# Group norm of the element after next, moved beside layer 1's last products

## The chip, the cores and the metric

The kernel runs on one core of a Trainium2 chip. A time is the device time of one execution in microseconds (us). The core has a matmul engine (PE, with a separate record of its weight loads, PEld), a vector engine (DVE), a scalar engine (ACT), a general engine (POOL) and a queue that issues the transfers (SP). Each engine works through its own list of instructions in order and waits on semaphores for the others. Matmuls write to PSUM, a small accumulation memory that PE, DVE and ACT use; everything else lies in SBUF, and the inputs and outputs in HBM.

## What is computed

The input x has 8 elements of 512 channels and 32 x 32 = 1024 positions, all in 32-bit floats. Two attention layers follow each other, element by element:

```python
# layer 0
hn  = group_norm(x, gn1_scale, gn1_bias)          # 32 groups of 16 channels
qkv = einsum('bchw,oc->bohw', hn, w_qkv) + b_qkv   # 8 heads of 64 channels
wgt = softmax(einsum('bct,bcs->bts', q * scale, k * scale))
a   = einsum('bts,bcs->bct', wgt, v)
x   = x + group_norm(einsum('bchw,oc->bohw', a, w_proj) + b_proj, gn2_scale, gn2_bias)
# layer 1: weights normalised by row, one head of 512 channels
qkv = einsum('oc,bcn->bon', w_qkv, x)
qkv = qkv / (sqrt(mean(qkv**2, axis=1)) + 0.0001)
attn = softmax(einsum('bci,bcj->bij', q, k) * C ** -0.5)
h   = einsum('oc,bcn->bon', w_out, einsum('bij,bcj->bci', attn, v))
out = (x + h) * 2 ** -0.5
```

The change concerns the first line, the group norm that makes `hn`, and where its work is done.

## The kernel before

Channels lie on the 128 partitions in 4 blocks (`CI` = 4), positions along the free dimension in two halves of 512 (`HN`). A matmul of 128 x 128 by 128 x 512 in 32-bit floats is recorded as two passes. The kernel keeps the order in which the program is written on every engine (`InOrder`, lines 26 to 34): nothing is reordered by a planner, and each engine's list is the order of the calls in the text.

The main loop (line 1012) goes over the elements b. Each starts with 32 **steps** of layer 0's heads (lines 1015 to 1058). A step i handles 128 query positions of two heads and is written in `Heads.step` (line 490): first the softmax of step i on DVE, ACT and POOL; then on PE, in odd steps from step 5 on, the values of an earlier pair of steps; then the step's *fill*, which in even steps is a piece of the projection of the next two heads' queries and keys (`project_rows`, tile `pqk`); then the scores of step i + 1 (tile `s`). After that come the transpose of the step before (`turn`, tile `pb`), its four transfers to `pT`, the work called *early*, the scaling by the sums (POOL), and the work called *later*.

Scores are made in halves: two heads of 64 channels each use half the rows of PE's array and run beside each other. One tile of scores is 128 x 1024 and fills two PSUM banks. The pool `ps_s` (line 101) has three such tiles, handed out in turn, two for each step; so the second head's scores of step i + 1 take the tile of the first head's scores of step i, once that head's exponential has read it. The pool `ps_m` (line 102) has two tiles of one bank, also in turn, for the values (`po`), the projection (`pqk`) and the small matmuls of the norms.

After the 32 steps, layer 0 is finished (`finish_layer0`), and layer 1 of the element is computed (`Layer1.project`, then `products`). Layer 1 ends with eight *products*: for each half `th` of the positions and each channel block c, eight matmuls of the weights e with the values v (`po<-e,v`, line 882), followed by `keep` (line 888), which on DVE divides by the softmax sums and adds x, and for the second half issues the output transfer. The four products of the first half stand by themselves (lines 1086 to 1092). The four of the second half are the fills of steps 0 to 3 of the next element's heads, ahead of the projection's piece where there is one (line 1097), and their `keep` is in the steps' later part.

The **norm** that makes `hn` of element b + 1 is spread over the heads of element b (lines 1034 to 1052): the four loads of 512 KB from HBM in steps 4 to 7, eight statistics on DVE in steps 6 to 13, their aggregation in step 14, then `GroupNorm.all_steps` one piece per step: a small matmul `pm` that averages over the groups, four small operations on DVE, a small matmul `pv` for the variance, and 17 small operations for the reciprocal root, the scale `a` and the offset `c`. POOL applies them to the four blocks in steps 21 and 22. `hn` of b + 1 is first read in step 24.

Large buffers are seven slots (`Slots`, line 37), handed out in the order in which they came free.

Of the kernel before, what the change touches and what calls it, by code (L numbers as in the profile page):

```python
# [13 lines left out]
P = 128  # L14
# [4 lines left out]
G1S, G1B, BQ, BK, BV, BP, G2S, G2B, GQKV, GOUT, NCOLS = 0, 4, 8, 12, 16, 20, 24, 28, 32, 44, 48  # L19
# [33 lines left out]
def attention_blocks_kernel(  # L53
# [26 lines left out]
    B, C, H, W = x.shape  # L80
    N = H * W
    NH, D, GROUPS = 8, C // 8, 32
    CI, NT, HN = C // P, N // P, N // 2
# [20 lines left out]
    PE, VE, AC, PO, SY = (InOrder(tc, e) for e in (nc.tensor, nc.vector, nc.scalar, nc.gpsimd, nc.sync))  # L104

    def big(name, lead=CI):

        return slots.take([P, lead, CI * N // lead], name)

    def wide(name):  # L110
        return ps_s.tile([P, 2, HN], F32, tag="sc", name=name)

    def bank(name, n=HN):
        return ps_m.tile([P, n], F32, tag="mm", name=name)

    def matmuls(pm, terms):

        for k, (lhsT, rhs) in enumerate(terms):
            PE.matmul(pm, lhsT, rhs, start=(k == 0), stop=(k == len(terms) - 1))
            if k % 2:  # L120
                yield

    def run(pieces):
        for _ in pieces:
            pass
# [4 lines left out]
    x0 = big("hn_0")  # L130
# [19 lines left out]
    def load_x(b, xt, ci):  # L150
        SY.dma_start(out=xt[:, ci, :], in_=xv[b, :, ci, :])
# [42 lines left out]
    def rsqrt_steps(r, v, n, name):  # L194

        t = small.tile([P, 4 * CI], F32, tag="rs_t", name=f"rs_{name}")[:, :n]
        VE.tensor_scalar(r.bitcast(I32), v.bitcast(I32), -0.5, 1597463007.0, ALU.mult, ALU.add)
        yield
        for _ in range(3):
            VE.tensor_mul(t, r, v)  # L200
            VE.tensor_mul(t, t, r)
            VE.tensor_scalar(t, t, -0.5, 1.5, ALU.mult, ALU.add)
            VE.tensor_mul(r, r, t)
            yield
# [29 lines left out]
    def fetch(name, b):  # L234
        SY.dma_start(out=place(name, b), in_=far[name])
# [19 lines left out]
    class GroupNorm:  # L255


        def __init__(self, mv, n, g0, b0, name):
            self.mv, self.n, self.g0, self.b0, self.name = mv, n, g0, b0, name

        def new(self, tag):
            return small.tile([P, CI], F32, tag=f"gn_{tag}", name=f"{tag}_{self.name}")[:, : self.n]

        def mean_steps(self):
            mv, n = self.mv, self.n
            pm = bank(f"pm_{self.name}")
            PE.matmul(pm[:, :n], gavg, mv[:, :, 0], start=True, stop=True)
            yield

            self.mean, self.d = self.new("mean"), self.new("d")  # L270
            VE.tensor_copy(self.mean, pm[:, :n])
            VE.tensor_sub(self.d, mv[:, :, 0], self.mean)
            VE.tensor_mul(self.d, self.d, self.d)
            VE.tensor_add(self.d, self.d, mv[:, :, 1])
# [3 lines left out]

        def coeff_steps(self):
            n = self.n  # L280
            pv = bank(f"pv_{self.name}")
            PE.matmul(pv[:, :n], gavg, self.d, start=True, stop=True)
            yield
            ve, self.a, self.c = self.new("ve"), self.new("a"), self.new("c")
            VE.tensor_scalar_add(ve, pv[:, :n], EPS)
            yield from rsqrt_steps(self.a, ve, n, self.name)
            VE.tensor_mul(self.a, self.a, cols[:, self.g0 : self.g0 + n])
            VE.tensor_mul(self.c, self.mean, self.a)
            VE.tensor_sub(self.c, cols[:, self.b0 : self.b0 + n], self.c)
# [10 lines left out]
    class Norm1:  # L300


        def __init__(self, b, xt):
            self.b, self.xt = b, xt
            self.st = small.tile([P, CI, 2, 6], F32, tag="gn_st1", name=f"st1_{b}")
            self.mv = small.tile([P, CI, 2], F32, tag="gn_mv1", name=f"mv1_{b}")
            self.gn = GroupNorm(self.mv, CI, G1S, G1B, f"1_{b}")

        def stats(self, ci, k):
            gn_stats(self.st[:, ci], self.xt[:, ci, :], k)  # L310
# [413 lines left out]
    class Layer1:  # L724
# [154 lines left out]
            PE.matmul(pe, root2, self.sums[th], start=True, stop=True)  # L879
            VE.reciprocal(self.sums[th], pe)  # L880

        def products(self, th, c):
            self.po = bank(f"po1_{self.b}_{th}_{c}")
            e = self.e[th]

            run(matmuls(self.po, [(self.v[:, t, c * P : (c + 1) * P], e[:, t, :]) for t in (0, 4, 1, 5, 2, 6, 7, 3)]))

        def keep(self, th, c):

# [54 lines left out]
    norm1 = Norm1(0, x0)  # L944
# [46 lines left out]
    v0_0 = big("v0_0", NT)  # L991
# [6 lines left out]
    qk0, todo = project_qk(0, 0, x0)  # L998
# [6 lines left out]
        slots.give(name)  # L1005


    heads = Heads(0, x0, v0_0, qk0)
    fills = [[lambda: next(v0)] for _ in range(CI)]
    laters = [[] for _ in range(CI)]  # L1010
    heads.scores(0)
    for b in range(B):
        hn, more = heads.hn, b + 1 < B
        todo = iter(())
        for i in range(STEPS):
            j, r = divmod(i, NB)
            due = []
            fill = [lambda: due.append(next(todo, None))] if (i - LAG) % RG else []
            early, later = [], []
            if i < CI:  # L1020
                fill, later = fills[i] + fill, laters[i]
            if r == 0:
                if j + 1 < CI:
                    heads.qk[j + 1], todo = project_rows(b, j + 1, hn)
                elif more:
                    qk_next, todo = project_rows(b + 1, 0, hn_next)
                if j + 1 == CI:
                    slots.give(f"hn_{b}")
                    if not more:
                        o_last = big(f"o_{b}")  # L1030
                        todo = project_out_half(b, heads, o_last)
            later.append(lambda: [f() for f in due if f])

            if more:


                if i == CI:
                    hn_next = big(f"hn_{b + 1}")
                    norm1 = Norm1(b + 1, hn_next)
                if 0 <= i - CI < CI:  # L1040
                    later.append(lambda: load_x(b + 1, hn_next, i - CI))
                if 0 <= i - CI - 2 < 2 * CI:
                    later.append(lambda: norm1.stats((i - CI - 2) // 2, i % 2))
                k = i - 3 * CI - 2
                if k == 0:
                    coeffs = norm1.gn.all_steps()
                    early += [norm1.aggregate, lambda: next(coeffs)]
                elif 0 < k < 8:
                    early.append(lambda: next(coeffs, None))
                if 0 <= k - 7 < CI // 2:  # L1050
                    for ci in range(2):
                        later.append(lambda ci=ci: norm1.apply(2 * (k - 7) + ci, PO))

            if i == STEPS - NB + 1:
                xt = big(f"x_{b}")
            if 0 <= i - (STEPS - NB + 1) < CI:
                later.append(lambda: load_x(b, xt, i - (STEPS - NB + 1)))
            heads.step(i, fill, early, later)

        if more:  # L1060
            v0_next = big(f"v0_{b + 1}", NT)
            v0 = project_v0(b + 1, hn_next, v0_next)
            next(v0)
        heads.values(STEPS // RG - 2)
        heads.turn()
        if more:
            fetch("proj7", b)
            ta = big(f"ta_{b}").rearrange("p (k i) (h n) -> p k i h n", k=2, h=2)
            rhs = RightSide(heads.a, ta[:, 0], ta[:, 1])
            for j in range(CI // 2 + 1):  # L1070
                rhs.sums(j)
            for _ in range(3):
                next(v0)
        else:
            fetch("score", b)
            begun = OutBegun(b, heads)
        heads.values(STEPS // RG - 1)
        slots.give(f"v0_{b}")
        if more:
            finish_layer0(b, heads, rhs, xt, v0)  # L1080
        else:
            finish_last(b, heads, xt, o_last, begun)
        fetch("value", b)
        one = Layer1(b, xt)
        one.project()
        for c in range(CI):
            one.products(0, c)
            if c == 0:
                one.total(0)
            one.keep(0, c)  # L1090
            if c == 1:
                one.total(1)
        slots.give(f"e_{b}_0")
        if more:
            heads = Heads(b + 1, hn_next, v0_next, qk_next)
            heads.scores(0)
            fills = [[lambda c=c: one.products(1, c)] for c in range(CI)]
            laters = [[lambda c=c: one.keep(1, c)] for c in range(CI)]

            def done(b=b):  # L1100
                for name in (f"v1_{b}", f"e_{b}_1", f"x_{b}"):
                    slots.give(name)

            laters[CI - 1].append(done)
        else:
            for c in range(CI):
                one.products(1, c)
                one.keep(1, c)
# [33 lines left out]
```

## Time and profile before

| | |
|---|---|
| median of 3 runs | 3293.95 us (3293.58 to 3295.57) |
| the profiled execution | 3295.35 us |
| its span, first to last instruction | 3293.2 us |
| granted clock of PE | 0.997 |
| busy: PE, DVE, ACT, POOL | 3263.8, 2118.5, 1071.5, 983.4 us |
| DVE, one statistic of 128 x 512 | 0.67 us |
| POOL, norm applied to one block of 128 x 1024 | 1.19 us |
| DVE, reciprocal of the sums, 128 x 512 | 3.35 us |
| load of one block of hn, issue to landing | 6.1 us |

A row of the profile names the engine, the operation, what is written and read (`out<-in`, buffer numbers left out), the shape and the count. `64*128` after MATMUL is a matmul that uses half of the array's rows. In an order of time each row has its start, counted from the first instruction, its length, and in brackets the idle time of the engine just before it with the releaser. Neighbouring rows of the same kind are merged (`x8`). The ends of matmuls are modelled, so the distance between the starts of two rows is the better measure of what a group costs.

### The profile page before, as it was taken

The numbers are of one execution on the slowest core, as the hardware profiler recorded it, in microseconds if no ns is written. First come the engines' busy times: TensorE is split into PE (matmuls) and PEld (weight loads), VectorE is DVE, ScalarE is ACT, GpSimd is POOL, SyncE is SP. The second block draws the span as 40 slices with busy tenths as digits, with TensorE's granted clock in tenths as the row PEclk, the third lists the DMA queues.
The fourth block names the chain that finished last, engine by engine and source line by source line (L and its number), as shares of the span: only waits on it lengthen the run. The fifth ranks groups of instructions, "written<-read, shape, count | busy, mean of one in ns | idle before, by whom it ended". The sixth has DMA issues, their size and how long they took to land.

```text
span 3293.2 us, 35605 instructions
## 1 busy us (share of the span) xinstructions
PE 3263.8 (99%) x13178; PEld 1606.6 (49%) x13178; DVE 2118.5 (64%) x2869; ACT 1071.5 (33%) x1813; POOL 983.4 (30%) x857
## 2 busy tenths in 40 slices
PE   8999999999999999999999999999999999999899
PEld 4444544545444454444544445444554545444354
DVE  4696647955488554885449754596645966468653
ACT  2453124521145211551215412254123531145210
POOL 0352123511245022460214503254122531235121
PEclk9999999999999999999999999999999999999899
DMA  5675206741078411782118811287204762057500
GB/s 189 195 196 166 81 6 179 202 150 67 8 205 212 128 45 35 209 219 91 45 53 216 233 52 44 81 219 208 77 13 125 207 177 90 13 140 196 183 7 26
DMA packets 182707, 410.82 MB, mean 125 GB/s; under 512 B 27620, under 2 KB 27656, under 8 KB 176520
## 3 DMA queue, kind: packets, MB, share of 16 engines
q1 hardware_dynamic: 182416, 408.53, 43.6%
q8 instruction: 105, 1.72, 0.2%
q14 instruction: 66, 0.54, 0.0%
q10 hardware_dynamic: 120, 0.02, 0.0%
HBM read 112.48 MB, written 27.56 MB: 43 GB/s over the span
## 4 chain that ended last, share of the span: by engine, by line
PE 94%; DVE 2%; DMA 2%; SPq 1%; issue 1%; DVEq 0%; ACTq 0%
PE po L34 26%; PE s L34 13%; PE pqk L34 12%; PE pv L34 7%; PE p_e_T L34 7%; PE p_e_B L34 5%; PE py L34 4%; PE p_u_T L34 3%; PE p_v_T L34 3%; PE p_o_T L34 3%; PE p_v_B L34 3%; PE p_u_B L34 3%; PE p_o_B L34 2%; DMA pT<-pb 1%; DVE pb L34 1%; PE pG L34 1%
## 5 line engine op out<-in xcount | busy, mean ns | idle before, releaser
L34 POOL TENSOR_SCALAR p<-p,tt 128x1024 f32<-128x1024 f32 x512 | 566.8, 1120 | 917.0 <-DVE tt L34 915.3
L34 ACT ACTIVATE p<-s,nm 128x1024 f32<-128x1024 f32 x512 | 565.9, 1110 | 839.6 <-DVE nm L34 801.1
L34 DVE TENSOR_REDUCE nm<-s 128x1 f32<-128x1024 f32 x512 | 602.1, 1217 | 180.1 <-PE s L34 179.2
L34 DVE STREAM_TRANSPOSE pb<-p 128x2048 f32<-128x2048 f32 x256 | 589.5, 2303 | 29.6 <-POOL p L34 18.8
L34 PE MATMUL s<-qk 64*128 64x512 f32 x2048 | 508.7, 602 | 0.0
L34 PE MATMUL po<-pT,v 128*64 128x256 f32 x4096 | 471.8, 383 | 3.8 <-DMA pT<-pb 2.8
L34 PE MATMUL pqk<-hn,qk 64*128 64x512 f32 (+1 forms) x2016 | 473.9, 591 | 0.0
L34 PE MATMUL po<-e,v 128*128 128x512 f32 x1024 | 450.9, 595 | 0.0
L34 PEld LDWEIGHTS po<-pT,v 128*64 128x64 f32 x4096 | 287.2, 137 | 217.1 <-ACT v L34 68.2
L34 PEld LDWEIGHTS pqk<-hn,qk 64*128 64x128 f32 (+1 forms) x2016 | 201.8, 187 | 252.1 <-issue 240.2
L34 PEld LDWEIGHTS po<-e,v 128*128 128x128 f32 x1024 | 192.2, 190 | 252.7 <-issue 245.5
L34 PEld LDWEIGHTS s<-qk 64*128 64x128 f32 x2048 | 194.4, 186 | 238.8 <-issue 234.2
L34 POOL TENSOR_TENSOR u<-u,xy 128x512 f32<-128x512 f32 x64 | 78.9, 1270 | 762.8 <-DMA xy<-far_rinv 390.2
L34 PE MATMUL pv<-v,hn 128*128 128x512 f32 x512 | 229.0, 598 | 0.0
L34 DVE TENSOR_TENSOR e<-e,p_e_T 128x512 f32<-128x512 f32 x160 | 107.0, 685 | 145.0 <-PE p_e_T L34 142.8
L34 POOL TENSOR_TENSOR qk<-qk,v 128x512 f32<-128x512 f32 x124 | 158.6, 1279 | 83.9 <-ACT v L34 83.9
L34 ACT ACTIVATE e<-e,shift,rinv 128x512 f32<-128x512 f32 x128 | 100.8, 811 | 247.7 <-DVE e L34 247.7
L34 POOL TENSOR_TENSOR esum<-esum,e 128x512 f32<-128x512 f32 x96 | 121.5, 1267 | 163.9 <-ACT e L34 161.4
L34 PEld LDWEIGHTS pv<-v,hn 128*128 128x128 f32 x512 | 94.6, 190 | 115.1 <-issue 114.8
L34 PE MATMUL p_e_T<-s,t 128*128 128x512 f32 x320 | 147.8, 592 | 0.0
L34 PE MATMUL py<-x,gram 128*128 128x512 f32 x320 | 141.6, 602 | 6.0 <-issue 6.0
L34 DVE TENSOR_TENSOR v<-po,esum 128x512 f32<-128x512 f32 x56 | 38.7, 691 | 160.0 <-PE po L34 159.8
(186 smaller groups left out, 3062.3 us busy)
## 6 DMA issues: line engine op xcount, KB each, us to landing
pT<-pb SPq DMA_DIRECT2D x1024, 256.0 KB, 4.4
hn<-in_x_dram SPq DMA_DIRECT2D x32, 512.0 KB, 6.1
x<-in_x_dram SPq DMA_DIRECT2D x32, 512.0 KB, 6.1
out_dram<-x SPq DMA_DIRECT2D x32, 512.0 KB, 3.3
score<-far_score SPq DMA_DIRECT2D x8, 1792.0 KB, 7.6
value<-far_value SPq DMA_DIRECT2D x8, 1792.0 KB, 7.0
qk<-far_qk SPq DMA_DIRECT2D x7, 2048.0 KB, 8.0
proj<-far_proj SPq DMA_DIRECT2D x7, 1792.0 KB, 9.1
```

What stands on the lines that cost most here:

```text
L34: return lambda *args, **kw: self._pin(call(*args, **kw))
```

## The change

Four things are done together.

1. For elements 2 to 7 the norm is moved out of the heads into the end of layer 1 of the element two before. After `project()`, the slot for `hn` of b + 2 is taken and its four loads are issued. The statistics and their aggregation come after the third product of the first half. The matmul `pm` is issued after half of the fourth product's matmuls, and `pv` after half of the next product's (`between`, `norm_step`). The norm of element 1 stays in the heads of element 0.
2. These small matmuls take a tile of the scores' pool (`wide`) and not of `ps_m`.
3. POOL applies the norm in steps 1, 3, 5 and 7 of the heads of element b, one block each.
4. The first product of the second half is issued before the heads of the next element begin, for every element but the last. The other three become the fills of steps 0 to 2; step 3's is empty. The slots of layer 1 are given back a step earlier.

```diff
-            pm = bank(f"pm_{self.name}")
+            pm = self.bank(f"pm_{self.name}")
...
-            pv = bank(f"pv_{self.name}")
+            pv = self.bank(f"pv_{self.name}")
...
-        def products(self, th, c):
+        def products(self, th, c, between=None):
...
-            run(matmuls(self.po, [(self.v[:, t, c * P : (c + 1) * P], e[:, t, :]) for t in (0, 4, 1, 5, 2, 6, 7, 3)]))
+            terms = [(self.v[:, t, c * P : (c + 1) * P], e[:, t, :]) for t in (0, 4, 1, 5, 2, 6, 7, 3)]
+            for k, _ in enumerate(matmuls(self.po, terms)):
+                if k == 1 and between:
+                    between()
...
-            if more:
+            if b and more and i % 2 and i < 2 * CI:
+                later.append(lambda: norm1.apply(i // 2, PO))
+            if not b:
...
         one = Layer1(b, xt)
         one.project()
+        hn_now, steps = hn_next, iter(())
+
+        def norm_step():
+            next(steps, None)
+
+        if b + 2 < B:
+
+            hn_next = big(f"hn_{b + 2}")
+            norm1 = Norm1(b + 2, hn_next, lambda name: wide(name)[:, 0])
+            for c in range(CI):
+                load_x(b + 2, hn_next, c)
+            steps = norm1.gn.all_steps()
         for c in range(CI):
-            one.products(0, c)
+            one.products(0, c, norm_step if c == CI - 1 else None)
             if c == 0:
                 one.total(0)
+            if c == 2 and b + 2 < B:
+                for ci in range(CI):
+                    for k in range(2):
+                        norm1.stats(ci, k)
+                norm1.aggregate()
+            if c == CI - 1:
+                norm_step()
             one.keep(0, c)
             if c == 1:
                 one.total(1)
         slots.give(f"e_{b}_0")
         if more:
-            heads = Heads(b + 1, hn_next, v0_next, qk_next)
+            one.products(1, 0, norm_step)
+            run(steps)
+            one.keep(1, 0)
+            heads = Heads(b + 1, hn_now, v0_next, qk_next)
             heads.scores(0)
-            fills = [[lambda c=c: one.products(1, c)] for c in range(CI)]
-            laters = [[lambda c=c: one.keep(1, c)] for c in range(CI)]
+            fills = [[lambda c=c: one.products(1, c)] for c in range(1, CI)] + [[]]
+            laters = [[lambda c=c: one.keep(1, c)] for c in range(1, CI)] + [[]]
...
-            laters[CI - 1].append(done)
+            laters[CI - 2].append(done)
```

More of the change, by code (lines that the diff above doesn't have):

```diff
@@ L255, in attention_blocks_kernel, with __init__ @@
     class GroupNorm:
-        def __init__(self, mv, n, g0, b0, name):
-            self.mv, self.n, self.g0, self.b0, self.name = mv, n, g0, b0, name
+        def __init__(self, mv, n, g0, b0, name, bank=bank):
+            self.mv, self.n, self.g0, self.b0, self.name, self.bank = mv, n, g0, b0, name, bank
         def new(self, tag):
@@ L300, in attention_blocks_kernel, with __init__ @@
     class Norm1:
-        def __init__(self, b, xt):
+        def __init__(self, b, xt, bank=bank):
             self.b, self.xt = b, xt
@@ L306, in __init__ @@
             self.mv = small.tile([P, CI, 2], F32, tag="gn_mv1", name=f"mv1_{b}")
-            self.gn = GroupNorm(self.mv, CI, G1S, G1B, f"1_{b}")
+            self.gn = GroupNorm(self.mv, CI, G1S, G1B, f"1_{b}", bank)
         def stats(self, ci, k):
@@ L1005, in attention_blocks_kernel @@
         slots.give(name)
-    heads = Heads(0, x0, v0_0, qk0)
+    heads, norm1, hn_next = Heads(0, x0, v0_0, qk0), None, None
     fills = [[lambda: next(v0)] for _ in range(CI)]
```

## The prediction

> **What bounds the kernel now.** I read the page's busy shares first, then the matmul engine's instructions in order of time around one boundary between two elements, then all engines in the same stretch.
>
> ```profile
> PE 3263.8 (99%) x13178; PEld 1606.6 (49%) x13178; DVE 2118.5 (64%) x2869; ACT 1071.5 (33%) x1813; POOL 983.4 (30%) x857
> PE 94%; DVE 2%; DMA 2%; SPq 1%; issue 1%; DVEq 0%; ACTq 0%
> ```
>
> PE is busy for all but 29 us, and those lie at the start and the end of the program. So nothing counts that does not change the number, the order or the waits of PE's instructions. PE in order of time, boundary from element 0 to element 1, steps 2 to 5 of element 1's heads (start us, length us):
>
> ```profile
> 915.85 4.12 PE L34 MATMUL pqk<-hn,qk 64*128 64x512 f32 x15
> 919.38 0.59 PE L34 MATMUL s<-qk 64*128 64x512 f32 x1
> 919.81 0.59 PE L34 MATMUL pqk<-hn,qk 64*128 64x512 f32 x1
> 919.81 2.30 PE L34 MATMUL s<-qk 64*128 64x512 f32 x7
> 922.04 7.13 PE L34 MATMUL po<-e,v 128*128 128x512 f32 x16
> 929.11 1.99 PE L34 MATMUL s<-qk 64*128 64x512 f32 x8
> 930.93 3.60 PE L34 MATMUL pqk<-hn,qk 64*128 64x512 f32 x16
> 934.36 1.88 PE L34 MATMUL s<-qk 64*128 64x512 f32 x8
> ```
>
> Step 3 is the 922.04 line: layer 1's last product (7.07 us to the next start), and then the scores of step 4. All engines in that stretch:
>
> ```profile
> 921.31 2.35 DVE L34 TENSOR_REDUCE nm<-s 128x1 f32<-128x1024 f32 x2 [3.94 <-PE s L34]
> 922.63 1.11 ACT L34 ACTIVATE p<-s,nm 128x1024 f32<-128x1024 f32 x1 [1.60 <-DVE nm L34]
> 923.58 2.30 DVE L34 STREAM_TRANSPOSE pb<-p 128x2048 f32<-128x2048 f32 x1
> ```
>
> The maximum of head 0's scores starts at 921.31, its exponential runs from 922.63 to 923.74. Scores have a ring of three PSUM tiles and two tiles per step, so the second head's scores of step 4 take the tile that this exponential empties. Today that is hidden: PE is in the product until 929.11.
>
> The norm's two small matmuls, in element 2's heads (first two lines), and the same pair for the second norm between full-array matmuls (last three):
>
> ```profile
> 989.53 0.39 PE L34 MATMUL pm<-mv,gavg 128*128 128x4 f32 x2
> 990.05 3.67 PE L34 MATMUL po<-pT,v 128*64 128x256 f32 x32
> ...
> 1128.25 0.28 PE L34 MATMUL pm<-mv,gavg 128*128 128x4 f32 x2
> 1128.39 3.68 PE L34 MATMUL pv<-v,hn 128*128 128x512 f32 x8
> 1131.90 0.28 PE L34 MATMUL pv<-d,gavg 128*128 128x4 f32 x2
> ```
>
> In the heads pm delays the next matmul by 0.52 us (990.05 - 989.53); in the full-array stretch by 0.14.
>
> [...] at 916.70 half the array waits 0.56 us for VectorE to free a bank, and no later work is taken in its place. [...] scores run as two 64-row halves, each half one pass per 0.429 us, and scores that follow a full-array product last 1.92 us up to another full-array product, 1.82 up to another 64-row stage. [...]
>
> **The change, part by part.** Sums are made against the profiled execution (3295.35 us, span 3293.2); the median of the three runs is 1.4 us under it, so I add the difference to 3293.95.
>
> *Small matmuls.* For elements 2 to 7 pm and pv leave the heads. From PE's order of time: pm costs 0.43, 0.52, 0.42, 0.49, 0.52 and 0.51 us in the heads of elements 1 to 6 (2.89), pv 0.32, 0.31, 0.32, 0.32, 0.31, 0.31 (1.89). At 0.14 each inside the products they cost 12 x 0.14 = 1.68. Gain 3.1 us, as long as their inputs are there. Bounds: 2 (if they cost as much as 0.22 there) to 3.5.
>
> *Are the inputs there?* hn of the element after next gets the slot of u, whose last reader on PE ends at 855.34, when the products begin. SP then issues four 512 KB loads; SP's issue of such a load takes 1.2 us, landing 6.1, so all are in by about 867. Nothing is queued behind them on SP until the first output at 893. On VectorE the statistics stand behind the reciprocal of the sums (871.47 to 874.82). Eight statistics take 4.76 us and four aggregates 0.4 at the start of the program, so mv is ready at 880.0. pm is reached at 881.1 (product 3 starts at 877.66, and half of it is 3.43). Margin 1.0 us. keep of product 2 comes behind the statistics and ends at 881.4; the product that needs its bank starts at 884.7. d (four operations of 0.2 us) is there at 882.3, pv wants it at 888.1. The 17 last operations take 3.3 us and end at 891.8, when keep of the next product is due, before the reduce at 893.7. So VectorE's part costs nothing; the products of 6.87 us each cover it. Were this cover short, PE would stop inside product 3, six times.
>
> *Heads.* VectorE loses the statistics, POOL's applies go from two pairs (2.37 us each) to one of 1.19 us in steps 1, 3, 5 and 7, SP loses four loads of 1.2 us and issues the first output of an element (0.34 us) one product earlier, with pT's transfers as its only neighbours. POOL has 2.2 us of scaling and at most 1.3 us of adding in a step of 5.3, and behind an apply only the next scaling waits. PE gains nothing: from step 5 to step 31 of element 1 (936.24 to 1075.81) it takes 139.57 us, which is 13 pairs at 10.67 plus pm and pv (0.86). There is no stall to remove.
>
> *The empty step.* At all seven boundaries one product of layer 1 now stands ahead of the scores of step 0, the other three move up one step, and step 3, which has no projection and no values, is left with nothing between scores 3 and scores 4. On the old clock: scores 3 start at 919.38, the exponential of head 0 ends at 923.74 (nothing ahead of it changes). PE restarts about 0.16 us after a releaser ends (VectorE's v ended at 916.64; counting back from 922.04 the half restarted at 916.80), so at 923.90, where without a wait it would go on at 921.95: a stall of 1.95 us. From there the waiting half has 4 passes of scores, 8 of projection, 4 of scores: 16 x 0.429 = 6.86, and 0.1 for the mode change: values start at 930.86, 11.48 after scores 3. Before: 936.17 - 919.38 = 16.79. The moved product costs 6.86 in its new place. Net per boundary 6.86 + 11.48 - 16.79 = +1.55; the saved pair of mode changes is in it. Seven times: +10.9 us. Behind the waiting scores in PE's queue stand the projection, scores 5 and the values. ACT needs scores 4 only at 927, and the next scores' exponential is done at 928.4, before PE asks at 929, so the wait doesn't repeat. Bounds: +0.6 (if half the wait is absorbed) to +2.6 (if step 4 or 5 waits once more).
>
> Sum: +10.9 - 3.1 = +7.8. 3293.95 + 7.8 = 3301.8 us, 0.24% slower.
>
> **Rivals.**
> *A: the empty step is free* (PE's halves rebalance, or the exponential comes in time). Then the boundary gives -0.4 instead of +1.55, 7 x -0.4 - 3.1 = -5.9: 3288 us. It speaks for it that only one half waits, against it that the exponential follows the scores by 3.25 us with no work between. It decides when the wait is under 0.85 us instead of 1.95.
> *B: statistics late.* If mv comes over 1.0 us later, PE waits inside product 3. Two us beyond it give 6 x 2 = 12: 3314 us. Against: loads have 7 us to spare. For: VectorE's queue has only 1.0.
> *C: the compressed steps run into the transfers of pT.* Transpose 4 needs the buffer of transpose 2, whose transfers take 3.2 us to issue and 4.4 to land: 932.8 against 933.2. One more us of stall per boundary gives 3309 us.
> *D: within the measurement*, the same mechanism but each stall 0.3 us shorter: 3299.7.
>
> **How the numbers follow.** 0.2% is 6.6 us, about what these runs can tell from no change: slower means over 3300.5. My value stands 1.3 us above that, and the size of one stall (seven times +-0.3) and of the small matmuls (+-1) is the uncertainty. Main case 0.55, of which most is above the line; D 0.27; A 0.06 (half of it beyond 0.2%); B 0.05; C 0.07. Slower: 0.48 of the main case with B and C: 0.60. Same: D, the rest of the main case and half of A, some 0.36. Faster 0.04. The range 3297 to 3307 leaves out A, B and part of C; the main case alone is 3300 to 3304.
>
> **What would show it.** In the profile after: scores 4 of elements 1 to 7 start straight after scores 3, with PE or its weight load idle near 2 us, released by ACT's p; values start some 11.5 us after scores 3; pm and pv at 0.14 us each in the products; no idle before pm; the step pairs still 10.67. It is wrong if PE shows no idle there, if pm waits for mv, or if the pairs of later steps get shorter.

## The result, and the profile after

The changed kernel takes 3305.19 us (median of 9 runs, 3303.09 to 3306.10) and the kernel before, run beside it, 3295.57: a ratio of 1.0029, with a 95% interval of 1.0019 to 1.0040. That is 0.3% slower, 9.6 us; the forecast was 7.8 us, with 3301.8 us as the time and 3297 to 3307 as the range.

The page's busy shares and the shares of the chain that ended last, after:

```profile
PE 3261.8 (99%) x13178; PEld 1603.1 (49%) x13178; DVE 2123.7 (64%) x2869; ACT 1073.0 (32%) x1813; POOL 982.8 (30%) x857
PE 98%; DVE 1%; DMA 0%; issue 0%; ACT 0%; SPq 0%; ACTq 0%; DVEq 0%
```

Nothing stands out here. PE is busy for 2 us less, in a span 10.2 us longer. What has changed shows in the list of who waited for whom, for PE (total us, times, longest us), whose first row did not exist before:

```profile
PE s L34 <- ACT p L34: 12.4, 7, 1.8
PE py L34 <- issue: 6.0, 1, 6.0
```

Scores wait seven times for the exponential, once at each boundary between elements. PE in order of time, at the boundary from element 1 to element 2, from the projection's piece in step 2 to the values of step 5:

```profile
926.29 4.12 PE L34 MATMUL pqk<-hn,qk 64*128 64x512 f32 x15
929.83 0.59 PE L34 MATMUL s<-qk 64*128 64x512 f32 x1
930.25 0.59 PE L34 MATMUL pqk<-hn,qk 64*128 64x512 f32 x1
930.26 2.31 PE L34 MATMUL s<-qk 64*128 64x512 f32 x9
934.33 1.55 PE L34 MATMUL s<-qk 64*128 64x512 f32 x5 [1.77 <-ACT p L34]
935.30 0.59 PE L34 MATMUL pqk<-hn,qk 64*128 64x512 f32 x1
935.72 0.59 PE L34 MATMUL s<-qk 64*128 64x512 f32 x1
935.73 3.59 PE L34 MATMUL pqk<-hn,qk 64*128 64x512 f32 x14
938.73 0.59 PE L34 MATMUL s<-qk 64*128 64x512 f32 x1
939.15 0.59 PE L34 MATMUL pqk<-hn,qk 64*128 64x512 f32 x1
939.16 2.30 PE L34 MATMUL s<-qk 64*128 64x512 f32 x7
941.39 3.67 PE L34 MATMUL po<-pT,v 128*64 128x256 f32 x32
```

The product that stood between scores 3 and scores 4 is gone. Ten passes of scores run on (the rows at 929.83 and 930.26), eight of step 3 and the first two of step 4, and then PE stands for 1.77 us. From the start of scores 3 (929.83) to the values (941.39) it is 11.56 us. The same stretch on DVE and ACT:

```profile
931.75 2.36 DVE L34 TENSOR_REDUCE nm<-s 128x1 f32<-128x1024 f32 x2 [3.94 <-PE s L34]
933.07 1.11 ACT L34 ACTIVATE p<-s,nm 128x1024 f32<-128x1024 f32 x1 [1.60 <-DVE nm L34]
```

The exponential ends at 934.18, and PE goes on 0.15 us later. Counted from scores 3, reduce and exponential start as early as before to 0.01 us (1.92 and 3.24 us); only the cover is missing.

The small matmuls and the end of the aggregation that they wait for, at the same boundary (DVE row first):

```profile
882.57 0.41 DVE L34 BATCH_NORM_AGGREGATE mv<-st 128x2 f32<-128x12 f32 x4
884.22 0.28 PE L34 MATMUL pm<-mv,gavg 128*128 128x4 f32 x2
884.36 7.11 PE L34 MATMUL po<-e,v 128*128 128x512 f32 x16
891.31 0.28 PE L34 MATMUL pv<-d,gavg 128*128 128x4 f32 x2
891.45 3.68 PE L34 MATMUL po<-e,v 128*128 128x512 f32 x8
```

mv is ready at 882.98, 1.2 us before PE comes to pm. Eight matmuls of a product take 6.87 us without a small one among them; from 884.36 to 891.31 they take 6.95. So a small matmul costs 0.14 us up to its successor's start and 0.08 after it.

Cut into stages (starts of rows on PE; "boundary" runs from the first matmul of the sums in layer 1 to the values of step 5, "heads" from there to layer 0's output projection, or to its counterpart in the last element):

| us | before | after |
|---|---|---|
| first matmul of the sums, element 0 | 463.42 | 465.21 |
| boundary to elements 1 to 6, each | 73.96 | 76.05 |
| boundary to element 7 | 73.96 | 75.60 |
| heads of elements 1 to 6 | 167.95 to 168.59, sum 1009.05 | 167.21, once 168.20, sum 1004.25 |
| heads of element 7 | 151.93 | 150.80 |
| rest of an element | 156.87 | 156.87 |

The boundaries cost 6 x 2.09 + 1.63 = 14.2 us, the heads of elements 1 to 6 give back 4.8, those of element 7 and its end 0.9, and 1.8 us are lost before the first boundary. The last two are probably not the change's doing. The start does the same work in both kernels, and in the six kernels below, whose starting code has the same order, that point lies between 463.5 and 465.3. And in the heads of element 7 the granted clock of the kernel before is 0.50 from 3077.96 to 3081.37, which the changed kernel's trace does not have. Without the start the change costs 8.4 us, without both 9.4.

### The profile page after: what moved, and what is told of

It is laid out like the page before. It is cut to its first block, busy times and chain, and to the rows that moved or that the text cites. A ratio compares the mean times of both kernels' runs of the same rounds, so it can differ in the third digit from the quotient of the medians.

```text
span 3303.4 us, 35653 instructions
## 1 busy us (share of the span) xinstructions
PE 3261.8 (99%) x13178; PEld 1603.1 (49%) x13178; DVE 2123.7 (64%) x2869; ACT 1073.0 (32%) x1813; POOL 982.8 (30%) x857
## 4 chain that ended last, share of the span: by engine, by line
PE 98%; DVE 1%; DMA 0%; issue 0%; ACT 0%; SPq 0%; ACTq 0%; DVEq 0%
PE po L34 27%; PE s L34 14%; PE pqk L34 14%; PE pv L34 7%; PE p_e_T L34 7%; PE p_e_B L34 5%; PE py L34 4%; PE p_u_T L34 3%; PE p_v_T L34 3%; PE p_o_T L34 3%; PE p_v_B L34 3%; PE p_u_B L34 2%; PE p_o_B L34 2%; PE pG L34 1%; PE pA L34 0%; PE pB L34 0%
## 5 line engine op out<-in xcount | busy, mean ns | idle before, releaser
L34 PE MATMUL s<-qk 64*128 64x512 f32 x2048 | 515.0, 603 | 12.4 <-ACT p L34 12.4
L34 ACT COPY v<-pv 128x1024 f32<-128x1024 f32 x32 | 32.2, 1007 | 259.4 <-PE pv L34 243.7
```

Of the source, the lines that this page charges most:

```text
L34: return lambda *args, **kw: self._pin(call(*args, **kw))
```

## The experiments

**Filling the empty step.** The changed kernel, with the projection's piece of step 2 issued in step 3:

```diff
-            fill = [lambda: due.append(next(todo, None))] if (i - LAG) % RG else []
+            piece = i in (0, 3, 4, 6) if b and i < NB else i % 2 == 0
+            fill = [lambda: due.append(next(todo, None))] if piece else []
```

> As the changed kernel, but from element 1 on the projection's piece of step 2 is issued in step 3, so that no step is empty. Theory (the stall between scores 3 and scores 4 is what the change costs): PE's wait for ACT's p disappears at all seven boundaries, and the wait for VectorE to free the bank in step 2 with it. Summed from the rows of before: scores 0 to the values of step 5 in 43.4 us where the changed kernel takes 46.3, so 7 x -2.9 = -20 us against the changed kernel, and about -11 us against the kernel before (ratio 0.9966). Rival (the moved norm is the cost, or the empty step is free): no more than the bank wait of 1 us per boundary goes, -7 us, still at or above the kernel before.

Measured: 3284.06 us (3282.89 to 3284.84) against 3295.97 for the kernel before; ratio 0.9964, interval 0.9951 to 0.9977. The row of scores waiting for ACT is gone from PE's waits, and the boundaries take 73.17 us (72.72 to element 7), 2.88 us less than in the changed kernel. PE in order of time from the product of step 2 on:

```profile
914.62 7.13 PE L34 MATMUL po<-e,v 128*128 128x512 f32 x16
921.69 1.99 PE L34 MATMUL s<-qk 64*128 64x512 f32 x8
923.51 3.60 PE L34 MATMUL pqk<-hn,qk 64*128 64x512 f32 x16
926.94 1.88 PE L34 MATMUL s<-qk 64*128 64x512 f32 x8
928.66 3.60 PE L34 MATMUL pqk<-hn,qk 64*128 64x512 f32 x16
932.09 1.88 PE L34 MATMUL s<-qk 64*128 64x512 f32 x8
933.91 3.67 PE L34 MATMUL po<-pT,v 128*64 128x256 f32 x32
```

The piece now follows scores, and with the scores behind it it takes 5.15 us (923.51 to 928.66). In step 2 of the kernel before, behind a product and waiting for a bank, the same two took 6.19 us (915.85 to 922.04). So one line removes the wait of step 2 and the stall of step 4; a like wait for a bank in step 0 stays (6.19 us from 899.45 to 905.64). This version is faster than either kernel.

**The products' new order alone.** The kernel before, with the norm left in the heads:

```diff
+            one.products(1, 0)
+            one.keep(1, 0)
             heads = Heads(b + 1, hn_next, v0_next, qk_next)
             heads.scores(0)
-            fills = [[lambda c=c: one.products(1, c)] for c in range(CI)]
-            laters = [[lambda c=c: one.keep(1, c)] for c in range(CI)]
+            fills = [[lambda c=c: one.products(1, c)] for c in range(1, CI)] + [[]]
+            laters = [[lambda c=c: one.keep(1, c)] for c in range(1, CI)] + [[]]
...
-            laters[CI - 1].append(done)
+            laters[CI - 2].append(done)
```

> The kernel before with part 4 of the change alone: the first product of the second half ahead of the heads, the others in steps 0 to 2, step 3 empty, and the norm left in the heads. Theory: the stall of about 1.8 us per boundary shows as in the changed kernel, +1.6 us each, +11.5 us in all (ratio 1.0035), the rest of the heads as before. Rival (the norm's move is the cost): within 3 us of the kernel before.

Measured: 3306.59 us, ratio 1.0033 (1.0020 to 1.0046). The boundaries take 75.60 us, all seven alike, 1.64 more than before; PE's wait list has the same row as the changed kernel's, 12.4 us in 7 waits. The whole loss comes from this part. The rival, that moving the norm costs time, falls.

**The small matmuls back in the heads.** The changed kernel, with loads, statistics and aggregation where it puts them:

```diff
-            if b and more and i % 2 and i < 2 * CI:
-                later.append(lambda: norm1.apply(i // 2, PO))
+            if b and more:
+                k = i - 3 * CI - 2
+                if k == 0:
+                    coeffs = norm1.gn.all_steps()
+                if 0 <= k < 8:
+                    early.append(lambda: next(coeffs, None))
+                if 0 <= k - 7 < CI // 2:
+                    for ci in range(2):
+                        later.append(lambda ci=ci: norm1.apply(2 * (k - 7) + ci, PO))
...
-            norm1 = Norm1(b + 2, hn_next, lambda name: wide(name)[:, 0])
+            norm1 = Norm1(b + 2, hn_next)
...
-            steps = norm1.gn.all_steps()
```

> The changed kernel with loads, statistics and aggregation where it puts them, but pm, pv and the small operations back in steps 14 to 21 of the heads, in the banks of the values, and the applies in steps 21 and 22. Theory: each boundary gives back 0.45 us, each head pays 0.75 to 0.85: about +2 us against the changed kernel, to be seen in the order of time and not in the total. Rival (small matmuls cost the same anywhere): no change of either stage's sum.

Measured: 3305.72 us, ratio 1.0030 (1.0018 to 1.0042), not to be told from the changed kernel by the total. The stages tell them apart: each boundary takes 75.60 us (0.45 less) and each of the heads of elements 1 to 6 167.84 (0.63 more). The difference is 6 x 0.18 = 1.1 us, about half of what was expected; the price of 0.75 to 0.85 us in the heads was too high. PE in the heads of element 2, where mv has been ready for a long time:

```profile
993.73 0.39 PE L34 MATMUL pm<-mv,gavg 128*128 128x4 f32 x2
994.05 3.67 PE L34 MATMUL po<-pT,v 128*64 128x256 f32 x32
1004.72 0.38 PE L34 MATMUL pv<-d,gavg 128*128 128x4 f32 x2
1005.04 3.67 PE L34 MATMUL po<-pT,v 128*64 128x256 f32 x32
```

pm costs 0.32 us here, like pv. In the kernel before, where VectorE writes mv in the same step, it took 0.42 to 0.52 us. The extra 0.1 to 0.2 us lies behind pm's start: in the heads of element 2 it starts 1.81 us after the scores before it in both kernels. In the next two experiments, where PE stands until mv is there, pm also takes 0.1 us more up to its successor (0.24 instead of 0.14). So an mv that has only just been written fits as the cause, but it was not tried apart.

**Statistics late.** The changed kernel, with the statistics behind `keep` of the third product:

```diff
             if c == 0:
                 one.total(0)
-            if c == 2 and b + 2 < B:
-                for ci in range(CI):
-                    for k in range(2):
-                        norm1.stats(ci, k)
-                norm1.aggregate()
             if c == CI - 1:
                 norm_step()
             one.keep(0, c)
+            if c == 2 and b + 2 < B:
+                for ci in range(CI):
+                    for k in range(2):
+                        norm1.stats(ci, k)
+                norm1.aggregate()
```

> The changed kernel with the statistics behind keep of the third product instead of ahead of it, which makes mv later by the wait for that product. Theory (a margin of about 1 us covers the statistics): keep ends at 882.3 on the changed kernel's clock, statistics and aggregation at 887.5, pm is due at 884.2, so PE stands still for about 3.4 us inside the fourth product at six boundaries: +20 us against the changed kernel (ratio to before 1.009). Rival (PE has other work there, or the statistics are far off the path): no change.

Measured: 3335.24 us, ratio 1.0117 (1.0102 to 1.0132): 30 us above the changed kernel, not 20. The stop is about as expected, 3.16 us at each of six boundaries, but those to elements 1, 3 and 5 take 79.47 us (3.42 more) and those to elements 2, 4 and 6 take 81.17 (5.12 more). PE at two of them, with its granted clock from the table of stretches (length, busy us of PE, PEld, DVE, ACT, POOL with the counts, then the granted clock, the transfers' share and GB/s):

```profile
889.91 0.39 PE L34 MATMUL pm<-mv,gavg 128*128 128x4 f32 x2 [3.15 <-DVE mv L34]
890.15 8.81 PE L34 MATMUL po<-e,v 128*128 128x512 f32 x16
...
1295.16 0.38 PE L34 MATMUL pm<-mv,gavg 128*128 128x4 f32 x2 [3.16 <-DVE mv L34]
1295.41 7.11 PE L34 MATMUL po<-e,v 128*128 128x512 f32 x16
```

```profile
890.00:894.00 4.00, 4.00 (x8) 1.80 (x9) 0.65 (x4) 0.00 (x0) 0.00 (x0) 0.61 0.00 0
1295.00:1299.00 4.00, 3.83 (x11) 1.92 (x12) 0.76 (x6) 0.00 (x0) 0.00 (x0) 1.00 0.00 0
```

After the first stop the clock is 0.61 in the mean of these 4 us (0.50 from 890.92 to 894.33 in the trace's record of the clock), and the same 16 passes last 8.81 us instead of 7.11. In the profiled execution (3330.16 us) this happened at the three boundaries that take longer. The other runs lie 5 us higher at a lower mean clock (0.994 instead of 0.996), so more clock was lost there; how it was divided among the boundaries is not known, as they have no trace.

**Statistics half late.** As the last one, with only the statistics of the last two channel blocks and the aggregation behind `keep`:

```diff
             if c == 2 and b + 2 < B:
-                for ci in range(CI):
+                for ci in range(CI // 2):
                     for k in range(2):
                         norm1.stats(ci, k)
-                norm1.aggregate()
             if c == CI - 1:
                 norm_step()
             one.keep(0, c)
+            if c == 2 and b + 2 < B:
+                for ci in range(CI // 2, CI):
+                    for k in range(2):
+                        norm1.stats(ci, k)
+                norm1.aggregate()
```

> The changed kernel with half of the statistics and the aggregation behind keep of the third product. Theory: keep ends at 882.3 on the changed kernel's clock, four statistics and the aggregation at 885.1, pm is due at 884.2: PE waits 0.9 us at six boundaries, each costing 1.0, +6 us against the changed kernel, with the granted clock as before. Rival (any stop inside a product costs clock as well, as three of six did when all statistics were late): 1.7 us more at some boundaries, +11 us or more.

Measured: 3310.25 us, ratio 1.0046 (1.0032 to 1.0059), 5 us above the changed kernel. All six boundaries take 77.10 us, 1.05 more than in the changed kernel, and the mean clock stays at 0.997:

```profile
885.44 0.39 PE L34 MATMUL pm<-mv,gavg 128*128 128x4 f32 x2 [0.78 <-DVE mv L34]
```

So the cover of the statistics is as thin as its margin says. Six stops of 0.78 us cost 1.05 us each and no clock.

**Filled step, norm in the heads.** The second experiment with the first one's line for the projection's piece.

> The reordered products with the projection's piece in step 3 as in the first experiment, but with the norm left in the heads as in the kernel before. It tells what the norm's move is worth once no step is empty. Theory: the boundary as in the first experiment less the two small matmuls (72.7 us), the heads 0.74 to 0.85 us longer: 6 x 0.3 = 2 us above the first experiment, ratio to before 0.997. Rival (VectorE, freed of the statistics, is what makes the heads faster): 5 us or more above the first experiment.

Measured: 3287.38 us, ratio 0.9974 (0.9965 to 0.9983), 3.3 us above the first experiment by the medians, which come from two chips. The boundaries take 72.72 us, the heads of elements 1 to 6 167.95 and once 169.16. Against the first experiment (73.17 and 167.21, once 168.21) each element pays 0.74 - 0.45 = 0.29 us: 1.7 us in all. That is what moving the norm is worth by itself once no step is empty; the rival of 5 us or more is not borne out by the stages.

## Why the prediction was right

- *Which elements the rows belong to.* The first boundary starts at 463.42, so the rows of the prediction from 855 to 936 are the boundary from element 1 to element 2, and the steps from 936.24 to 1075.81 are element 2's; the prediction names these an element too early (the heads at 989.53 are rightly element 2's). All seven boundaries take 73.96 us, so no sum depends on it.
- *PE is the bound, and only its instructions, their order and their waits count.* Right. The statistics and the loads left the heads, and the step pairs are 10.67 us as before.
- *The empty step stalls on the ring of three score tiles.* Right in place, releaser and number (seven, ACT's p). PE goes on 4.50 us after scores 3 start (929.83 to 934.33), 4.52 forecast; the forecast stall of 1.95 is counted from where the half would have gone on, 2.57 us after scores 3 start, and so counted 1.93 were measured, while the 1.77 of the wait list begins at the modelled end of the last pass. Scores 3 to the values 11.48 forecast (with 0.1 for the mode change, an estimate from the 1.92 and 1.82 us of scores), 11.56 measured; net per boundary +1.55 forecast, +1.64 measured without the small matmuls (second experiment). Filling the step removes it. Rival A falls.
- *The wait doesn't repeat.* Right, but not by much: the next first exponential ends at 938.70, and the waiting scores begin at 939.16. Rival C did not come at the boundaries.
- *Small matmuls at 0.14 us in the products.* This term was mis-sized: 0.225 each (0.45 per boundary, 76.05 against 75.60). The forecast took the time to the next row's start alone; 0.08 more lies in the row after it, and could have been read before (3.51 us from 1128.39 to 1131.90 for eight passes that take 3.43). It makes 1.0 us in all, and the upper cost named beside the sum, 0.22, was the right one.
- *Small matmuls removed from the heads: 4.78 us.* (The pm of element 4 is 0.45 by its rows, 1787.70 to 1788.15, and not 0.49.) The heads' sum fell by 4.8, which agrees partly by luck. In the second experiment, with the norm in the heads, most heads take 167.95, 0.74 above 167.21, so 4.4 us belong to the norm; the rest is pauses that come and go. One such pause, in the changed kernel's heads of element 2:

```profile
1074.37 2.31 DVE L34 STREAM_TRANSPOSE pb<-p 128x2048 f32<-128x2048 f32 x1 [2.47 <-DMA pT<-pb]
1079.20 0.30 PEld L34 LDWEIGHTS s<-qk 64*128 64x128 f32 x4 [0.71 <-ACT p L34]
```

  The transpose waits 2.47 us for transfers of pT, while loads of x are issued (at 1067.67 and 1073.78), and the delay passes through the exponential to the same ring of score tiles: these heads take 1.0 us more. "There is no stall to remove" in the heads was therefore not quite right; it was read from element 2's heads, which have almost none (168.04). Above 167.95 the kernel before has 0.4 us in the heads of element 3 and 0.6 in those of element 6.
- *The inputs are there in time.* Right: mv 1.2 us ahead of pm (1.0 forecast), coefficients done at 894.98, before `keep` at 895.17. The two experiments with late statistics show that rival B's mechanism is real and that the margin decides.
- The sum: boundaries +11.5 (10.9 forecast), small matmuls in the products +2.7 (1.7), heads -4.8 (-4.8), together +9.4; element 7 and the end gave 0.9 back and the start took 1.8, neither of which the prediction's steps have, and which half cancel by luck. The time itself is 3.4 us over the forecast 3301.8: 1.8 us by the change, and 1.6 because the kernel before came out at 3295.57 and not at 3293.95.

## What to carry to other kernels

Where work is taken out of a step that covered a dependence, look at what then stands next to what in the bound engine's list: here two groups of scores, whose ring of tiles allows them side by side only if a reduce and an exponential (2.4 us) fit between. Count such a gap with the ring's depth before moving anything, and spread what is left evenly over the steps; one piece moved from a full step to the empty one turned a loss of 0.3% into a gain of 0.36%. What an operation costs on a full engine is the shift of everything behind it, read two rows further on, and not its own row.

## What was not expected of the hardware

Six equal stops of PE of 3.15 to 3.16 us in the middle of dense matmuls were followed, at three of the boundaries, by a lower granted clock, shown above for the first of them (0.61 in the mean of 890 to 894 us). It cost 1.69 us more each time: the 16 passes behind the stop last 8.81 us in the rows at 890.15, 1699.01 and 2507.82, and 7.11 in those at 486.60, 1295.41 and 2104.26. The stops of 1.77 us in the changed kernel (clock 1.00 from 500 to 3084 us) and those of 0.78 us in the experiment with the statistics half late (mean clock 0.997, all six boundaries 77.10 us) were not followed by one.

The length of a stop alone does not tell which it will be. In the heads of element 7 PE has one long wait for pT in every trace. In the kernel before, that stop is 2.83 us long, the clock behind it is 0.50 (3078.00 to 3081.40), and the 32 values at 3078.29 last 5.18 us. In the changed kernel it is longer, 3.19 us, and yet the clock behind it is 1.00 (3084 to 3094), and the same row, at 3089.79, lasts 3.67. In the experiments the row lasts 3.67 us behind one stop of 2.84 us (small matmuls back in the heads) and 4.98 to 5.30 behind five of 2.60 to 3.14 us. What else decides is not shown: no run was made to tell.
